# Bias columns by wide products, an earlier iota, and stores on another queue in a two-layer attention kernel

## Chip, cores and metric

The kernel runs on one core of a Trainium2 chip, in one launch. The metric is the device time of that launch in microseconds (us); of several runs the median is taken. Everything is float32.

## What is computed

Two layers follow each other on x, 8 images of 32 x 32 positions with 512 channels (8 x 1024 tokens).

```python
# layer 0
x_norm = group_norm(x) * gn_scale + gn_bias
q, k, v = split(x_norm @ w_qkv + b_qkv)                 # 8 heads of 64
x = x + softmax(q k^T / 64) v @ w_out + b_out
...
# layer 1, on the tokens as 4-dimensional image
q = layernorm(x) @ wq + bq
o = gelu(depthwise_7x7_stride_2(q) + dw_b)              # 16 x 16 points
offsets = pw_w o
interp = bilinear samples of x at (reference points + tanh(offsets))   # 256 rows
v = interp @ wv + bv
k = interp @ wv + bv
qh, kh, vh = q @ mq_w + mq_b, k @ mk_w + mk_b, v @ mv_w + mv_b
z = softmax(qh kh^T) vh @ mo_w + mo_b + x
out = gelu(layernorm(z) @ mlp_w + mlp_b) + z
```

Two matrix products in a row, such as wv and then mk_w, are folded by the kernel into one matrix (wvk = wv mk_w) with one bias. The bias of the folded key product is mk_b + mk_w^T bv, a vector of 512; it is kept as four columns on 128 partitions (512 = 4 x 128). There are three such vectors: bvk (keys: mk_w with bv), bvv (values: mv_w with bv) and bqq (queries: mq_w with bq).

## The kernel before, in words

**Layer 0** goes through 8 batches; a batch has 4 pairs of heads with 8 query tiles each, so 32 units per batch (`per`). A unit (`push`, line 205) makes the scores of one query tile and one pair of heads on TensorE (two PSUM tiles "sc"), their row maxima on VectorE ("nmax"), the exponentials on ScalarE ("e"), and two 32x32-block transposes of them on VectorE into "sq". After every second unit 16 DMAs on SP's queue move "sq" into "et" (`moved`, line 221), and TensorE multiplies "et" by the values some units later ("av"). VectorE scales that by the inverse row sums into "attT".

All other work is put between units by a list of due steps: `at(place, step)` (line 375) enters a step at a place, and `run_due(until)` (line 378) runs all steps due in order of place. It is called twice per unit n: with n + 0.8 after the unit's scores, maxima and exponentials and before its transposes, and with n + 1 after the transposes. `InOrder` keeps every engine's instructions in the order in which they are so recorded: an engine waits at the first instruction that isn't ready. Every instruction recorded this way has line 54 in the profile, so groups are known by their tiles.

Between units lie the next batch's group norm and q, k, v products, the output product of the batch before (`out_steps`, line 703: product with w_out, "xr" as the residual sum, statistics, then layernorm into "hat", stored as hat_d for layer 1), and a part of layer 1: the depthwise convolution, by taps that VectorE adds into "od" and by taps that ScalarE multiplies into two buffers "part_x" and GpSimd adds into "oa" (`conv_chunk`, line 884).

**The last batch (7).** `fold_steps` (line 794) folds the weights. At unit 18.3 `load_biases` (line 429) issues eight loads of small vectors on GpSimd's queue; at 18.4 `set_refs` (line 440) writes partition numbers by an iota on GpSimd and makes reference points of them in eight small VectorE operations. The products for wvk lie at 25.5 to 29.5, for wvv at 30.5 to 32.52, for wqq after the last unit. `add_cols` (line 319) makes the bias columns: for each of 4 output chunks and 4 input chunks one product with a 128x128 weight and a single moving column, 16 products of 128x1, and four ScalarE additions of one column. It is called for bvk at 29.55, for bvv at 35.5 and for bqq at 36.6 (32 is the batch's end).

The last batch's output steps have their own places (`last_places`, line 781): output tiles 0 to 3 are made and normed first, tiles 4 to 7 at 36.2 to 36.35 with norms at 36.84 and after. In this batch the norms run on VectorE (three operations of 128x512 each) and the stores to mid and to hat_d are issued by GpSimd.

**Layer 1** has 16 half batches of 4 pairs of heads. `prep` (line 1062) fetches the first normed tokens, copies two bias vectors for wide products ("rep_w"), gathers the 4 x 2 sets of 128 sample rows of batch 0 by indirect DMAs of GpSimd ("row", four buffers), weighs and adds them on VectorE ("smp"), loads the late weights on SP's queue, and makes the first query product (`query_step(0, 0)`), the keys of four pairs and the values. `unit_steps` (line 1261) then records each unit; 0.042 after unit n stands the query product of unit n + 1.

Three lines show how a wide product is made before, in `project` (line 361), which the rest of the kernel uses: for each of 4 input chunks two halves of 64 output partitions, a moving operand of 512 columns.

```python
for c in range(NC):
    for m in range(2):
        nc.tensor.matmul(out[half], lhsT=lhsT(c)[:, half], rhs=rhs(c), start=(c == 0), stop=(c == NC - 1))
```

Of the kernel before, what the change touches and what calls it, by code (L numbers as in the profile page):

```python
# [9 lines left out]
F32 = mybir.dt.float32  # L10
I32 = mybir.dt.int32
AF = mybir.ActivationFunctionType
ALU = mybir.AluOpType
AX = mybir.AxisListType
# [3 lines left out]
P = 128  # L18
# [3 lines left out]
C = 512  # L22
NC = C // P
NT = S // P
# [223 lines left out]
def attention_then_deformable_attention(  # L248
# [48 lines left out]
    def mm_tile():  # L297
        return ps_mm.tile([P, QB], F32, tag="mm", name="mm")
# [17 lines left out]
        nc.sync.dma_start(t, v.partition_broadcast(P))  # L316
        return t

    def add_cols(dst, w, vec, on_scalar=False):

        n = dst.shape[1]
        ps = mm_tile()
        for o in range(n):
            for c in range(NC):
                nc.tensor.matmul(
                    ps[:, o : o + 1],
                    lhsT=w[:, c, ts(o, P)],
                    rhs=vec[:, c : c + 1],
                    start=(c == 0),
                    stop=(c == NC - 1),  # L330
                )
        if on_scalar:
            for o in range(n):
                col = dst[:, o : o + 1]
                nc.scalar.activation(col, ps[:, o : o + 1], AF.Identity, bias=col)
        else:
            nc.vector.tensor_tensor(dst, ps[:, 0:n], dst, ALU.add)

    def repeat(pool, vec, bufs):

# [34 lines left out]
    def at(place, step):  # L375
        due.append((place, len(due), step))
# [52 lines left out]
    def load_biases():  # L429
        with nc.allow_non_contiguous_dma(reason="small vectors onto partitions"):  # L430
# [4 lines left out]
            for o in range(2):  # L435
                nc.gpsimd.dma_start(
                    pww[:, :, o], pw_w[o].rearrange("(c p) a b -> p (c a b)", p=P)
                )

    def set_refs():  # L440
        nc.gpsimd.iota(pid, pattern=[[0, 1]], base=0, channel_multiplier=1)
        nc.vector.tensor_scalar(rc[:, 0:1], pid, 4, None, ALU.logical_shift_right)
        nc.vector.tensor_scalar(rc[:, 1:2], pid, G - 1, None, ALU.bitwise_and)
        for h in range(2):
            nc.vector.tensor_copy(refs[:, h, :], rc)
        nc.vector.tensor_scalar(refs[:, 1, 0:1], refs[:, 1, 0:1], float(P // G), None, ALU.add)
        nc.vector.tensor_scalar(refs, refs, 0.5, 2.0 / G, ALU.add, ALU.mult)
        nc.vector.tensor_scalar(refs, refs, -1.0, None, ALU.add)
# [61 lines left out]
    with ExitStack() as l0:  # L510
# [192 lines left out]
        def out_steps(b, attT, places, last=False):  # L703

            src = x_tok[b].rearrange("(t p) c -> p t c", p=P)
            dst = mid[b].rearrange("(t p) c -> p t c", p=P)

            room = {}
            to_mid, to_hat = [nc.gpsimd if last else nc.sync] * 2
            by = nc.vector if last else nc.gpsimd

            def row(name, t):

                if last and name == "hat":
                    tag, bufs = ("q", 3) if t < NQT else ("v", 5)
                    return work.tile([P, C], F32, tag=tag, name=name, bufs=bufs)
                if last and t >= NQT + NX:  # L720
                    return (conv["bq"], conv["part"].rearrange("p a s -> p (a s)"))[t % 2]
                if last and t >= NQT:
                    return work.tile([P, C], F32, tag="x", name=name, bufs=NX)
                return work.tile([P, C], F32, tag="xr", name=name, bufs=4)

            def fetch(t):
                room[t] = row("xr", t)
                nc.gpsimd.dma_start(room[t], src[:, t, :])

            def add(t):  # L730
                nc.gpsimd.tensor_tensor(room[t], room[t], bout, ALU.add)

            def out(t):
                room["ps", t] = project(
                    lambda c: attT[c, t // NQT][:, ts(t % NQT, P)], lambda c: room_w["w"][:, c, :]
                )

            def summed(t):
                xr = room[t]
                nc.vector.tensor_tensor(xr, room["ps", t], xr, ALU.add)  # L740
                to_mid.dma_start(dst[:, t, :], xr)
                stats = work.tile([P, 6], F32, tag="stats1", name="stats1", bufs=2)
                mv = room["mv", t] = work.tile([P, 3], F32, tag="mv1", name="mv1", bufs=4)
                nc.vector.bn_stats(stats, xr)
                nc.vector.bn_aggr(mv[:, 0:2], stats)
                rstd(mv[:, 2:3], mv[:, 1:2], 1e-5)

            def norm(t):
                xr, mv = room[t], room["mv", t]
                hat = row("hat", t)  # L750
                nc.vector.tensor_scalar(
                    hat, xr, mv[:, 0:1], mv[:, 2:3], ALU.subtract, ALU.mult
                )
                by.tensor_tensor(hat, hat, lng_row, ALU.mult)
                by.tensor_tensor(hat, hat, lnb_row, ALU.add)
                to_hat.dma_start(hat_d[b][:, t, :], hat)

            for t in range(NT):
                for place, what in zip(places[t], (fetch, add, out, summed, norm)):
                    at(place, lambda t=t, what=what: what(t))  # L760
# [33 lines left out]
        def fold_steps(first):  # L794

            raws, wT = {}, {}

            def spare():
                return work.tile([P, NC, QB], F32, tag="xT", name="raw", bufs=NX_T)

            def fetch(name, w):
                raws[name] = spare()
                nc.gpsimd.dma_start(raws[name], by_chunk(w))

            def turn(name, m):
                if name == "v" and m == 0:
                    wT[name] = spare()
                src = room_w["w"] if name == "v" else raws["wq"]
                ps = mm_tile()
                for c in range(NC):  # L810
                    nc.tensor.transpose(ps[:, ts(c, P)], src[:, c, ts(m, P)], ident)
                nc.scalar.copy(wT[name][:, m, :], ps)

            def product(dst, tag, name, raw, i):
                if i == 0:
                    fold[dst] = kept(tag)
                ps = project(lambda m: wT[name][:, m, ts(i, P)], lambda m: raws[raw][:, m, :])
                nc.scalar.copy(fold[dst][:, i, :], ps)

            at(first + 18.3, load_biases)  # L820
            at(first + 18.4, set_refs)
            at(first + 17.7, lambda: load_weight(wv))
            at(first + 19.3, lambda: fetch("mk", mk_w))
            for m in range(NC):
                at(first + 23.5 + m // 2 + 0.05 * (m % 2), lambda m=m: turn("v", m))
            at(first + 25.3, lambda: load_weight(w_out))
            at(first + 26.7, lambda: fetch("mv", mv_w))
            for i, place in enumerate((25.5, 27.5, 28.5, 29.5)):
                at(first + place, lambda i=i: product("wvk", "wC", "v", "mk", i))
            at(first + 29.55, lambda: add_cols(bvk, raws["mk"], bv_c, on_scalar=True))  # L830
            at(first + 29.7, lambda: fetch("wq", wq))
            for i, place in enumerate((30.5, 31.5, 32.5, 32.52)):
                at(first + place, lambda i=i: product("wvv", "wB", "v", "mv", i))
            last = first + per
            at(last + 0.6, lambda: wT.update(q=spare()))
            at(last + 3.5, lambda: add_cols(bvv, raws["mv"], bv_c, on_scalar=True))
            at(last + 3.6, lambda: fetch("mq", mq_w))
            for m in range(NC):
                at(last + 4.27 + 0.001 * m, lambda m=m: turn("q", m))
            for i in range(NC):  # L840
                at(last + 4.5 + 0.01 * i, lambda i=i: product("wqq", "wA", "q", "mq", i))
            at(last + 4.6, lambda: add_cols(bqq, raws["mq"], bq_c, on_scalar=True))

        def head_steps(first):

# [185 lines left out]
    with ExitStack() as l1:  # L1031
# [30 lines left out]
        def prep():  # L1062
            fetch_hat(0)
            load_small()
            fetch_hat(1)
            reps.extend(repeated(vec) for vec in (bvv, lnb))
            room[0, "ii"], room[0, "wt"] = head["ii"], head["wt"]
            for h in range(2):
                gather(0, h)
                sample(0, h)  # L1070
            for pad in pads:
                nc.gpsimd.memset(pad, 0.0)
            load_late()
            query_step(0, 0)
            for hp in range(NHP):
                key_step(0, hp)
            for t in range(2):
                value_step(0, t)
# [182 lines left out]
        def unit_steps(n):  # L1261
# [20 lines left out]
            last = n + 1 == 2 * B * NHP  # L1282
            at(n + (1.3 if last else 1.1), lambda: att.product(u))
            at(n + (1.305 if last else 1.2), scale)
            if not last:
                at(n + 0.042, lambda: query_step(*divmod(n + 1, NHP)))


# [114 lines left out]
```

## Time and profile before

| | us |
|---|---|
| three runs: lowest, median, highest | 3339.33, 3346.2, 3357.7 |
| the profiled execution's own time | 3348.16 |
| its span in the profile | 3346.5 |
| TensorE busy | 3273.1 |
| VectorE busy | 2494.1 |
| ScalarE busy | 1809.5 |
| GpSimd busy | 1544.3 |
| mean granted clock of TensorE | 0.993 of full speed |

How to read what is shown below. A timeline row has the start in us from the span's start, the time that a run of like instructions took, the engine, the line, the operation, output<-input by tile names, partitions x elements, and how many; in square brackets stands how long the engine had been idle before, and what ended that wait. One float32 product is two records of TensorE, so 16 records are the 8 instructions of one wide product. A row by stretches begins with the stretch, then its length, and the busy time and number of instructions of PE, PEld (weight loads), DVE, ACT and POOL; the three last columns are the granted TensorE clock, the share of the DMA engines and GB/s. "SPq" is SP's DMA queue. A wait for several semaphores is put down to the one that came last.

### The profile page before, as it was taken

To read this page: it belongs to the slowest core of one execution; us is meant where nothing else is said; L and a number is where in the kernel's file an instruction comes from. 1 tells how busy PE (TensorE), PEld (TensorE's weight loads), DVE (VectorE), ACT (ScalarE), POOL (GpSimd) and SP (SyncE) were. 2 spreads that over 40 slices of the span, in tenths; PEclk is the share of its full clock that TensorE was granted. 3 is DMA by queue.
4 is the path that set the end of the run, shared out by engine and by line. 5 is a ranking of instruction groups with operands and counts; after the bars stand their busy time and mean duration, and the time that the engine had idled before them with its cause. 6 is when DMAs were issued, how large, how long until landed. Compare 5 with 4: busy or idle time off the path is not lost.

```text
span 3346.5 us, 59638 instructions
## 1 busy us (share of the span) xinstructions
PE 3273.1 (98%) x21736; PEld 1337.3 (40%) x21736; DVE 2494.1 (75%) x3389; ACT 1809.5 (54%) x3927; POOL 1544.3 (46%) x1909
## 2 busy tenths in 40 slices
PE   7999999999999999999999999999999999999998
PEld 3344444344344344444444434433333333333333
DVE  5777788888898898888888877448767686665754
ACT  3443356576566567567567555135565555554442
POOL 1001226746745764764664663415455454642222
PEclk9999999999999999999999999999999999999999
DMA  5666766766776777766776767567566665665754
GB/s 151 176 181 163 209 181 180 232 180 181 208 202 180 214 195 183 208 193 184 212 193 176 201 185 214 163 196 221 185 208 202 192 201 189 212 216 191 226 181 130
DMA packets 441412, 643.61 MB, mean 192 GB/s; under 512 B 73152, under 2 KB 236992, under 8 KB 439072
## 3 DMA queue, kind: packets, MB, share of 16 engines
q1 hardware_dynamic: 409232, 531.93, 55.2%
q0 software_dynamic: 31888, 107.88, 10.5%
q8 instruction: 172, 2.82, 0.4%
q14 instruction: 120, 0.98, 0.1%
HBM read 247.43 MB, written 123.73 MB: 111 GB/s over the span
## 4 chain that ended last, share of the span: by engine, by line
PE 85%; ACT 4%; DVE 3%; DMA 3%; POOL 2%; issue 2%; SPq 1%; POOLq 0%; DVEq 0%; ACTq 0%
PE mm L54 54%; PE sc L54 16%; PE av L54 15%; ACT e L54 2%; SPq L54 1%; DMA et<-sq 1%; DVE nmax L54 1%; DVE sq L54 1%; POOL chunk L54 1%; DMA inv<-rs_d 1%; POOL xr L54 1%; DMA row<-mid,ii 0%; ACT L54 0%; DMA w<-in_L_conv_w_out_dram 0%; DVE smp L54 0%
## 5 line engine op out<-in xcount | busy, mean ns | idle before, releaser
L54 ACT ACTIVATE e<-sc,nmax 128x1024 f32<-128x1024 f32 (+1 forms) x1024 | 803.0, 797 | 480.9 <-DVE nmax L54 479.2
L54 DVE TENSOR_REDUCE nmax<-sc 128x1 f32<-128x1024 f32 (+1 forms) x640 | 751.5, 1215 | 344.5 <-PE sc L54 343.9
L54 POOL TENSOR_TENSOR oa<-part_x,oa 128x256 f32<-128x256 f32 x852 | 640.4, 752 | 553.7 <-ACT part_x L54 507.5
L54 DVE STREAM_TRANSPOSE sq<-e 128x1024 f32<-128x1024 f32 x640 | 766.2, 1228 | 156.8 <-ACT e L54 135.7
L54 ACT ACTIVATE part_x<-pad_x,dww_x 128x256 f32<-128x256 f32 x852 | 441.2, 545 | 259.4 <-POOL oa L54 257.9
L54 PE MATMUL sc<-k,q 64*64 64x512 f32 x4096 | 516.1, 605 | 15.8 <-ACT e L54 13.7
L54 PE MATMUL av<-et,v 128*64 128x256 f32 x4096 | 499.2, 386 | 6.2 <-DMA et<-sq 3.8
L54 PEld LDWEIGHTS av<-et,v 128*64 128x64 f32 x4096 | 273.4, 137 | 324.1 <-issue 164.5
L54 POOL TENSOR_TENSOR chunk<-parts,chunk 128x256 f32<-128x256 f32 x240 | 189.2, 788 | 259.3 <-ACT parts L54 245.3
L54 POOL TENSOR_TENSOR mv<-mv,minus_half 128x1 f32<-128x1 f32 x128 | 76.4, 597 | 462.8 <-DVE mv L54 462.0
L54 PEld LDWEIGHTS sc<-k,q 64*64 64x64 f32 x4096 | 139.4, 133 | 322.5 <-issue 208.4
L54 PE MATMUL mm<-xT,wB 128*64 128x512 f32 x1024 | 233.0, 597 | 3.2 <-issue 3.2
L54 DVE SCALAR_TENSOR_TENSOR od<-pad_x,dww_x,od 128x256 f32<-128x256 f32 x276 | 231.5, 839 | 5.5
L54 PE MATMUL mm<-wo,attH 128*64 128x512 f32 x1024 | 233.7, 598 | 0.0
L54 PE MATMUL mm<-w,attT 128*64 128x512 f32 x1024 | 232.5, 598 | 0.8 <-DMA w<-in_L_conv_w_out_dram 0.8
L54 PE MATMUL mm<-hat_h,wA 128*64 128x512 f32 x1024 | 232.9, 597 | 0.0
L54 PE MATMUL mm<-wC,xT 128*64 128x256 f32 x2048 | 232.1, 379 | 0.0
L54 PE MATMUL mm<-wm,zT 128*64 128x512 f32 x1024 | 230.7, 592 | 1.0 <-ACT zT L54 1.0
L54 PE MATMUL mm<-xT,wA 128*64 128x512 f32 x1024 | 230.7, 592 | 0.0
L54 ACT ACTIVATION_READ_ACCUMULATOR e<-sc,nmax 128x1 f32 x1024 | 209.2, 204 | 0.0
L54 ACT ACTIVATE parts<-pad,dww 128x256 f32<-128x256 f32 x240 | 126.5, 552 | 126.6 <-POOL chunk L54 125.6
L54 PEld LDWEIGHTS mm<-wC,xT 128*64 128x64 f32 x2048 | 148.1, 137 | 77.6 <-issue 6.4
(185 smaller groups left out, 3501.6 us busy)
## 6 DMA issues: line engine op xcount, KB each, us to landing
et<-sq SPq DMA_DIRECT2D x2048, 128.0 KB, 2.8
sq_d<-sq SPq DMA_DIRECT2D x128, 512.0 KB, 2.7
et<-sq_d SPq DMA_DIRECT2D x128, 512.0 KB, 4.5
inv<-rs_d SPq DMA_DIRECT2D x256, 128.0 KB, 4.6
hat_h<-hat_d SPq DMA_DIRECT2D x16, 1024.0 KB, 8.7
xr<-mid SPq DMA_DIRECT2D x64, 256.0 KB, 5.9
xr<-in_x_dram POOLq DMA_DIRECT2D x62, 256.0 KB, 3.9
x<-in_x_dram POOLq DMA_DIRECT2D x60, 256.0 KB, 4.5
```

The costliest lines, as they stand in the source:

```text
L54: return self.tc.keep_in_program_order(op(*args, **kwargs))
```

## The change

Four things are edited.

1. The iota gets a step of its own, `number`, at 18.3, ahead of the bias loads (now 18.35); the VectorE part, `set_refs`, goes to 19.3.
2. `add_cols` is replaced by `add_diagonal`. The two vectors bv and bq are each repeated over 128 columns by one VectorE copy (`repeats`, at 27.9; a tile [128, 8, 128] in the buffer of "hat_x"). A bias is then one wide product (`project`) of the repeated vector with the weight: every one of the 128 output rows holds all 512 values. VectorE multiplies it by the identity, repeated four times, into "own" (a "v" buffer), sums each block of 128 into "col", and adds that to the bias.
3. The stores of the last batch's normed tiles 4 to 7 are issued by ScalarE instead of GpSimd.
4. The query product of layer 1's unit 1 is recorded in `prep`, behind that of unit 0 and ahead of the keys, and left out after unit 0.

```diff
-    def add_cols(dst, w, vec, on_scalar=False):
-
-        n = dst.shape[1]
-        ps = mm_tile()
-        for o in range(n):
-            for c in range(NC):
-                nc.tensor.matmul(
-                    ps[:, o : o + 1],
-                    lhsT=w[:, c, ts(o, P)],
-                    rhs=vec[:, c : c + 1],
-                    start=(c == 0),
-                    stop=(c == NC - 1),
-                )
-        if on_scalar:
-            for o in range(n):
-                col = dst[:, o : o + 1]
-                nc.scalar.activation(col, ps[:, o : o + 1], AF.Identity, bias=col)
-        else:
-            nc.vector.tensor_tensor(dst, ps[:, 0:n], dst, ALU.add)
+    def add_diagonal(pool, dst, w, rep):
+
+        out = project(lambda c: rep[:, c, :], lambda c: w[:, c, :])
+        own = pool.tile([P, C], F32, tag="v", name="own", bufs=5).rearrange("p (o q) -> p o q", q=P)
+        nc.vector.tensor_tensor(
+            own, out.rearrange("p (o q) -> p o q", q=P),
+            ident.unsqueeze(1).to_broadcast([P, NC, P]), ALU.mult,
+        )
+        col = pool.tile([P, NC], F32, tag="mu", name="col", bufs=2)
+        nc.vector.tensor_reduce(col, own, AX.X, ALU.add)
+        nc.vector.tensor_tensor(dst, col, dst, ALU.add)
...
+    def number():
+        nc.gpsimd.iota(pid, pattern=[[0, 1]], base=0, channel_multiplier=1)
+
     def set_refs():
-        nc.gpsimd.iota(pid, pattern=[[0, 1]], base=0, channel_multiplier=1)
...
-                to_hat.dma_start(hat_d[b][:, t, :], hat)
+                (nc.scalar if last and t >= NQT else to_hat).dma_start(hat_d[b][:, t, :], hat)
...
+            def repeats():
+                both = work.tile([P, NT, P], F32, tag="hat_x", name="rep_b", bufs=1)
+                for half, vec in enumerate((bv_c, bq_c)):
+                    rep = raws["rep", half] = both[:, ts(half, NC), :]
+                    nc.vector.tensor_copy(rep, vec.unsqueeze(2).to_broadcast([P, NC, P]))
...
-            at(first + 18.3, load_biases)
-            at(first + 18.4, set_refs)
+            at(first + 18.3, number)
+            at(first + 18.35, load_biases)
+            at(first + 19.3, set_refs)
+            at(first + 27.9, repeats)
...
-            at(first + 29.55, lambda: add_cols(bvk, raws["mk"], bv_c, on_scalar=True))
+            at(first + 29.55, lambda: add_diagonal(work, bvk, raws["mk"], raws["rep", 0]))
...
-            at(last + 3.5, lambda: add_cols(bvv, raws["mv"], bv_c, on_scalar=True))
+            at(last + 3.5, lambda: add_diagonal(work, bvv, raws["mv"], raws["rep", 0]))
...
-            at(last + 4.6, lambda: add_cols(bqq, raws["mq"], bq_c, on_scalar=True))
+            at(last + 4.6, lambda: add_diagonal(work, bqq, raws["mq"], raws["rep", 1]))
...
             query_step(0, 0)
+            query_step(0, 1)
...
-            if not last:
+            if not last and n:
                 at(n + 0.042, lambda: query_step(*divmod(n + 1, NHP)))
```

## The prediction

> **What bounds the kernel now.** I read the busy table and the chain's shares first, then the timelines of TensorE (PE), VectorE (DVE), GpSimd (POOL) and ScalarE (ACT) around the edited steps (1.98 to 2.24 ms), then the granted clock by stretch.
>
> ```profile
> span 3346.5 us, 59638 instructions
> PE 3273.1 (98%) x21736; PEld 1337.3 (40%) x21736; DVE 2494.1 (75%) x3389; ACT 1809.5 (54%) x3927; POOL 1544.3 (46%) x1909
> ...
> PE 85%; ACT 4%; DVE 3%; DMA 3%; POOL 2%; issue 2%; SPq 1%; POOLq 0%; DVEq 0%; ACTq 0%
> ```
>
> TensorE is busy 98% of the span, so an edit counts only by what it does to TensorE's work, its idle stretches and its clock. All edits lie in the last batch of the first layer and the step to the second. There TensorE has two long idle stretches:
>
> ```profile
> 2003.50 4.30 PE L54 MATMUL sc<-k,q 64*64 64x512 f32 x16 [7.19 <-ACT e L54]
> ...
> 2185.42 9.84 PE L54 MATMUL mm<-smp,wC 128*64 128x256 f32 x60 [5.53 <-DVE smp L54]
> ```
>
> The first goes back over ScalarE's exponentials to VectorE, which waits for the iota behind eight bias loads:
>
> ```profile
> 1983.83 2.35 DVE L54 TENSOR_REDUCE nmax<-sc 128x1 f32<-128x1024 f32 x2 [0.33 <-PE sc L54]
> 1996.03 0.21 DVE L54 TENSOR_SCALAR rc<-pid 128x1 int32<-128x1 int32 x2 [9.85 <-POOL pid L54]
> ...
> 1994.35 1.49 POOL L54 DMA_DIRECT2D pww<-in_L_conv_pw_w_dram  x2
> 1995.84 0.15 POOL L54 IOTA pid<- 128x1 int32 x1
> ...
> 1996.72 0.53 ACT L54 ACTIVATE part_x<-pad_x,dww_x 128x256 f32<-128x256 f32 x1 [6.10 <-POOL oa L54]
> 2002.24 1.11 ACT L54 ACTIVATE e<-sc,nmax 128x1024 f32<-128x1024 f32 x1 [4.99 <-DVE nmax L54]
> ```
>
> The third thing to see is the clock (next to last columns: granted clock as a share, DMA share). TensorE is "busy" in the 128x1 products, yet the clock falls to half in and after them:
>
> ```profile
> 2075.66 3.60 PE L54 MATMUL mm<-raw 128*64 128x512 f32 x16
> 2079.19 4.24 PE L54 MATMUL mm<-bv_c,raw 128*128 128x1 f32 x32
> 2083.36 3.69 PE L54 MATMUL sc<-k,q 64*64 64x512 f32 x16
> 2086.98 2.96 PE L54 MATMUL av<-et,v 128*64 128x256 f32 x16
> ...
> 2079.20:2083.40 4.20, 4.20 (x38) 4.19 (x36) 0.00 (x0) 0.59 (x1) 0.00 (x0) 0.86 0.68 163
> 2083.40:2087.00 3.60, 3.60 (x19) 0.78 (x18) 0.00 (x0) 0.71 (x4) 1.84 (x3) 0.50 0.83 162
> ```
>
> **Part 1: iota ahead, refs one unit later.** The iota issues at about 1989.9, where the loads began (its 0.15 us goes ahead of their 5.96). VectorE no longer waits; what is late next? Its first conv tap into "od" needs the previous store of that tile, issued 1984.08 and landed 8.6 us later, at 1992.7. Two taps and the row maximum then end at 1994.7. But ScalarE's exponential stands behind a conv tap (1996.72) that waits for GpSimd's adds, still behind the same loads: it ends at 1997.4. So the first exponential runs 1997.4 to 1998.4 and TensorE resumes at 1998.45 instead of 2003.50: idle 2.2 us, not 7.2. The scores that follow ran at clock 0.58 and took 4.30 us; after an idle of 1.89 us (at 2064.8) the trace shows the usual 1.95, so I take full clock. They still need the second exponential (1999.55), so they end near 2001.3 instead of 2007.8, 6.5 earlier. The refs' eight small operations (1.7 us) now stand between maxima and transposes, where VectorE waits for the exponential anyhow; but three taps ahead of the next maxima delay its second exponential to 2007.4 where TensorE wants it at 2006.9, 0.5 lost. **Net -6.0**; bounds -7.4 (all idle but 2.2, full clock) and 0 (rival 2).
>
> **Part 2: bvk by a wide product.** 32 narrow records take 4.17 us to the next start (2079.19 to 2083.36); the same weights' wide product of 16 records takes 3.53 (2075.66 to 2079.19): 0.64 less. The products after it took 3.62 and 2.79 instead of 1.87 and 1.78, 2.8 more by the clock. Face value -3.4. But the diagonal is summed on VectorE, and in the changed order its three operations stand **ahead of the unit's two transposes**. They wait for the product's end, 2082.7. Masked multiply as other PSUM additions of 128x512 (0.69), reduction as half of a 1024-wide maximum (0.6), addition 0.16, gaps: 1.6 us. The transposes thus end at 2086.8 instead of 2078.94. Sixteen et<-sq transfers are queued on SP behind them; they were issued 2079.00 to 2090.36 and would end issuing near 2098.2, the last landing at 2100.4 to 2102.4 (2.8 to 4.8 from issue to landing, medians of the page and of 2100-2104). TensorE, now earlier, asks for them at 2097.4; before it began that product at 2100.87. So about 3.7 us of new idle, and the product begins at 2101.1: +0.2 in place of -3.4. An idle of 3.7 lies between 1.89 (no drop) and 5.53 (drop to 0.50); nearest in kind are the narrow products, where the clock fell after 2.5 to 3.2 us of thin work. I take a drop, 2.4 us (4.30 against 1.9 above). **Net +2.6**; bounds -3.4 (transfers in time) and +4.3 (last landing, 2.8 by the clock).
>
> [...]
>
> **Part 3: bvv, bqq, the stores and the early query, one chain.** Times are those of before, shifted as a whole by parts 1 and 2. Narrow bvv costs 4.59 us and 2.3 of slow clock after; wide 3.53. Its column sum now stands on VectorE ahead of the last attT scaling (which moves from 2132.8 to 2136.7; the output product needs it for its last quarter at 2137, so no idle) and of four norms (1.91 each). The norms' delay reaches back through the residual sums to TensorE by less than 1 us, so the wqq products start some 2.2 us earlier than 2155.0 and bqq's product ends at 2170.5 instead of 2173.8.
>
> Here is the new wait. Before, the four later norms ran 2156.97 to 2164.7, while TensorE made wqq:
>
> ```profile
> 2164.61 0.42 DVE L54 COPY rep_w<-bvv 128x512 f32<-128x512 f32 x1
> ...
> 2169.88 0.48 DVE L54 TENSOR_SCALAR smp<-row,wt 128x512 f32<-128x512 f32 x1 [4.51 <-DMA row<-mid,ii]
> ...
> 2184.61 0.75 DVE L54 SCALAR_TENSOR_TENSOR smp<-row,wt,smp 128x512 f32<-128x512 f32 x1 [0.96 <-DMA row<-mid,ii]
> ```
>
> Now bqq's column sum stands ahead of them and waits for 2170.5. Behind it: sum 1.6, norms 7.64, two copies 0.76, so sampling starts at 2180.6 instead of 2169.88. That POOL is free of the four stores lets only the first gather go early; the second is behind a buffer that the first norm reads. All four first-half rows are there by 2180.6, but the second four need their buffers back (2181.1 to 2183.5), are issued 2181.4 to 2185.3 at 1.3 apart, and the last lands 3.4 (first gather of before) to 8.2 us (its last, beside the weight loads) later. Those loads shift too: SP's first waits for the last norm's input and two others for ScalarE's stores. I take 5.7: sampling ends at 2191.8, TensorE's key products start 6.3 late (bounds 4.0 and 8.8). The query product put ahead, 3.53 us, fills idle time: -3.53. Later its absence is felt: it stood between the first scores and the first output product, which now comes 14.4 us after those scores began, while its second et landed 16.1 after them (2218.2 less 2202.05): +1.7. The slow restart (clock 0.50) is there in both. ScalarE's four stores hold back its query evacuations to 2180.6, ahead of the keys; an issue there is not in the trace, SP's 0.34 and POOL's 0.55 bound it, and it hides. **Net +4.5**, bounds -1.8 (sampling no later) and +7.1.
>
> **Sum.** -6.0 + 2.6 + 4.5 = +1.1 us on the profiled execution's 3348.16 (span 3346.5 and 1.7 around it), which stands 2.0 above the median of three, 3346.2. Forecast **3347**.
>
> **Rivals.**
> 1. *The column sums' queueing on VectorE decides* (slower). Place: norms and sampling behind bqq's sum, transposes behind bvk's. Price: +7.1 and +4.3, with the first stall's clock still dropping (-6.0 becomes -3.6): +7.8, 3354. It decides once the last gather lands over 6 us after issue and both idles drop the clock. For it: 8.2 measured beside the loads; against: these have partly drained by then. 0.25.
> 2. *The moved iota does nothing*: the chain names a late et<-sq as what released the transposes at 1997.95. Against it: the same kind of transpose started at 1970.44 amid its predecessor's transfers. Then 0 + 2.6 + 4.5: 3353. 0.10.
> 3. *The new waits hide*, savings stay: -6.0 - 3.4 - 1.8 = -11.2, 3335. For it: transfers of 2.8 us, earlier first gather; against: the queue order. 0.13.
>
> **How the numbers follow.** Likeliest 0.52. All cases lie within 0.4%; this kernel's measurement tells about 0.5% (17 us) from no change, and the three runs span 18 us. Range by the parts' bounds: 3334 (-12.6) to 3357 (+11.4). Faster 0.03, same 0.93, slower 0.04.
>
> **What would show it.** Right: idle before the scores near 2003 falls to about 2 us; VectorE waits some 6 us for TensorE ahead of the bvk sum and 15 us ahead of bqq's; TensorE idles ahead of an av product on et<-sq, and over 12 us ahead of the keys. Wrong: no such idle (rival 3), the 7 us still there (rival 2), or a shift in the second layer's steady units, where I expect none.

## The result, and the profile after

| kernel | median, us (runs) | lowest, highest | ratio to before, 95% interval |
|---|---|---|---|
| before | 3345.15 (20) | 3339.33, 3357.7 | |
| changed | 3354.53 (20) | 3344.81, 3360.48 | 1.0026 [1.0017, 1.0035] |

The change costs 9.4 us by the medians, 0.26%. The profiled execution of the changed kernel took 3351.23 us; it lies 3.3 below its kernel's median, and that of before (3348.16) lies 3.0 above its own. So the two traces, compared below, show a difference of 3.1 us where the medians show 9.4.

From the profile of the changed kernel: the span, the busy table and the shares of the chain of work that ended last, by engine.

```profile
span 3349.5 us, 59538 instructions
...
PE 3268.0 (98%) x21688; PEld 1328.8 (40%) x21688; DVE 2498.3 (75%) x3400; ACT 1806.6 (54%) x3915; POOL 1539.6 (46%) x1905
...
PE 86%; DVE 3%; ACT 3%; DMA 2%; POOL 2%; issue 2%; SPq 1%; POOLq 0%; ACTq 0%; DVEq 0%
```

TensorE is busy 5.1 us less (3273.1 before), and the span is 3.0 longer: the time went into idle stretches. The timeline of TensorE in the changed kernel shows which:

```profile
1997.81 3.04 PE L54 MATMUL sc<-k,q 64*64 64x512 f32 x16 [2.06 <-ACT e L54]
...
2061.25 3.36 PE L54 MATMUL av<-et,v 128*64 128x256 f32 x16 [2.54 <-DMA et<-sq]
...
2097.56 3.68 PE L54 MATMUL av<-et,v 128*64 128x256 f32 x16 [3.83 <-DMA et<-sq]
...
2168.75 7.04 PE L54 MATMUL mm<-hat_h,wA 128*64 128x512 f32 x32
2181.80 1.12 PE L54 MATMUL mm<-smp,wC 128*64 128x256 f32 x4 [6.01 <-DVE smp L54]
2191.60 8.48 PE L54 MATMUL mm<-smp,wC 128*64 128x256 f32 x60 [8.68 <-DVE smp L54]
```

The idle of 7.19 us before the scores is 2.06 now. In its place stand 3.83 us ahead of an output product, which did not exist before, and 14.69 us (6.01 and 8.68) ahead of the key products, where there were 5.53. VectorE's timeline says what it did meanwhile:

```profile
2078.99 0.69 DVE L54 TENSOR_TENSOR own<-mm,ident 128x512 f32<-128x512 f32 x1 [6.38 <-PE mm L54]
...
2168.97 0.69 DVE L54 TENSOR_TENSOR own<-mm,ident 128x512 f32<-128x512 f32 x1 [15.34 <-PE mm L54]
2169.69 0.69 DVE L54 TENSOR_REDUCE col<-own 128x4 f32<-128x512 f32 x1
2170.41 0.16 DVE L54 TENSOR_TENSOR bqq<-col,bqq 128x4 f32<-128x4 f32 x1
2170.50 0.54 DVE L54 TENSOR_SCALAR hat<-xr,mv 128x512 f32<-128x512 f32 x1
...
2178.81 0.48 DVE L54 TENSOR_SCALAR smp<-row,wt 128x512 f32<-128x512 f32 x1
...
2190.79 0.75 DVE L54 SCALAR_TENSOR_TENSOR smp<-row,wt,smp 128x512 f32<-128x512 f32 x1 [0.36 <-DMA row<-mid,ii]
```

VectorE stands still for 15.34 us, until TensorE has made the bqq product, and only then begins the four norms ("hat<-xr,mv"), whose inputs were complete by 2154.3. Sampling ("smp") follows the norms. GpSimd, too, waits for them, though its stores are gone from its queue:

```profile
2154.96 1.07 POOL L54 DMA_INDIRECT row<-mid,ii  x1 [0.49 <-issue]
2171.31 1.31 POOL L54 DMA_INDIRECT row<-mid,ii  x1 [15.28 <-DVE hat L54]
...
2184.03 0.95 POOL L54 DMA_INDIRECT row<-mid,ii  x1 [0.30 <-issue]
```

The first gather goes at once; the second needs a buffer that the first norm reads, and waits 15.28 us for it. In the kernel before, the gathers stood behind the four stores, and the first went later than the changed kernel's first, but earlier than its second:

```profile
2166.48 1.05 POOL L54 DMA_INDIRECT row<-mid,ii  x1 [0.70 <-issue]
```

Along TensorE's timeline the shift against before (negative: the changed kernel is earlier) is -0.6 us at the last scores that no edit can have touched (1989.04 to 1988.47), -6.9 at the output product after the first stall (2007.73 to 2000.79), -3.8 at the scores of 2072.01 (2068.25), -0.9 at the output product of 2109.51 (2108.66), +4.0 at layer 1's third scores (2228.64 to 2232.60), and +3.1 at the end. The first and the last but one of these places, in the timelines of before and then of the changed kernel:

```profile
1989.04 1.95 PE L54 MATMUL sc<-k,q 64*64 64x512 f32 x16
...
2228.64 1.96 PE L54 MATMUL sc<-keys,q 64*64 64x256 f32 x32
```

```profile
1988.47 1.95 PE L54 MATMUL sc<-k,q 64*64 64x512 f32 x16
...
2232.60 1.96 PE L54 MATMUL sc<-keys,q 64*64 64x256 f32 x32
```

What lies between them is called the edited stretch below. It is 4.5 us longer in the changed kernel's trace.

### The profile page after: what moved, and what is told of

Read it like the earlier page. It is cut to its first block, busy times and chain, and to the rows that moved or that the text cites. A ratio compares the mean times of both kernels' runs of the same rounds, so it can differ in the third digit from the quotient of the medians.

```text
span 3349.5 us, 59538 instructions
## 1 busy us (share of the span) xinstructions
PE 3268.0 (98%) x21688; PEld 1328.8 (40%) x21688; DVE 2498.3 (75%) x3400; ACT 1806.6 (54%) x3915; POOL 1539.6 (46%) x1905
## 3 DMA queue, kind: packets, MB, share of 16 engines
q0 software_dynamic: 31568, 106.83, 10.4%
## 4 chain that ended last, share of the span: by engine, by line
PE 86%; DVE 3%; ACT 3%; DMA 2%; POOL 2%; issue 2%; SPq 1%; POOLq 0%; ACTq 0%; DVEq 0%
PE mm L54 54%; PE sc L54 16%; PE av L54 16%; ACT e L54 2%; SPq L54 1%; POOL chunk L54 1%; DMA et<-sq 1%; DVE nmax L54 1%; DVE sq L54 1%; DMA inv<-rs_d 1%; POOL xr L54 0%; ACT L54 0%; DVE smp L54 0%; DMA et<-sq_d 0%; POOL res L54 0%
```

## The experiments

Theory A: VectorE takes its instructions in order (in the changed kernel it stood 15.34 us at bqq's sum with four norms behind it whose inputs were complete), so the place of the column sums decides; ahead of the transposes (bvk) and of the norms (bqq) they cost more than the earlier iota brings. Rivals: the stores on ScalarE's queue and the early query cost the time; the moved iota gives its gain back; the clock alone makes the difference.

All measured, each against before on the same chip (differences of medians). The last column is from the traces: how much longer the edited stretch is than in the profile of before. It rests on one execution of each kernel, but what happens in the rest of the program does not enter it.

| kernel | us against before | ratio, 95% interval | edited stretch, us |
|---|---|---|---|
| refs only | -7.5 | 0.9979 [0.9969, 0.9988] | -9.0 |
| wide products only | +18.9 | 1.0054 [1.0041, 1.0067] | +15.2 |
| stores and early query only | -11.7 | 0.9964 [0.9951, 0.9977] | -8.3 |
| changed, bqq's sum behind the norms, bvk's behind the transposes | -0.5 | 0.9992 [0.9983, 1.0001] | -11.5 |
| changed, with the narrow products of before | -14.9 | 0.9950 [0.9937, 0.9963] | -17.6 |
| changed, both sums behind (bqq's behind the first sampling) | -19.2 | 0.9939 [0.9926, 0.9952] | -19.1 |
| the same, bvk's sum ahead | -15.2 | 0.9953 [0.9940, 0.9966] | -15.8 |
| changed, again | +4.3 | 1.0018 [1.0004, 1.0032] | +7.0 |
| both sums behind, without the early query | -19.6 | 0.9943 [0.9928, 0.9958] | -18.8 |
| wide products only, both sums behind | -1.7 | 0.9998 [0.9989, 1.0007] | -7.0 |
| both sums behind, again | -18.2 | 0.9945 [0.9932, 0.9957] | -19.3 |
| stores only | -8.9 | 0.9972 [0.9960, 0.9984] | -10.9 |

Median and trace agree within 4 us, but for two kernels: the first attempt at placing the sums (-0.5 and -11.5) and the wide products with both sums behind (-1.7 and -7.0). The profiled execution of each of these two is the shortest of its kernel (as it is of three others). For the changed kernel's first comparison the two are +9.4 and +4.5.

### Each part alone

**Refs only.** Before, with

```diff
-            at(first + 18.3, load_biases)
-            at(first + 18.4, set_refs)
+            at(first + 18.3, number)
+            at(first + 18.35, load_biases)
+            at(first + 19.3, set_refs)
```

> The kernel before with the first part of the change alone: iota ahead of the bias loads, refs one unit later. Theory A (the change loses its time because the column sums stand ahead of other VectorE work; the moved iota itself gains): about 6 us less than before (ratio 0.998), idle before the scores near 2003 about 2 us instead of 7.2. Rival R1 (the moved iota is itself followed by a clock drop that takes half of its gain back, as the drop near 2061 in the changed kernel's profile suggests): about 3 us less. Rival R2 (medians of this kernel wander by 6 us with the clock, whatever is edited): no sign of its own, between -6 and +6 us.

Measured -7.5 us: theory A, and not half of it as R1 had. The idle ahead of the scores is 2.06 us here as well.

**Wide products only.** Before, with `add_diagonal` and `repeats` in the places that the change gives them.

> The kernel before with the three bias columns as wide products alone (iota, stores and second query as before). Theory A: slower, by +2.6 us at bvk and about +6 at the keys (VectorE's norms and sampling behind bqq's sum, no early query to fill the idle), less some 2 us for bvv: +5 to +9 us, with TensorE idle over 12 us ahead of the key products. Rival R3 (the stores on ScalarE's queue and the early query bring the loss): this kernel is faster, -3 to -6 us, by the shorter products and the full clock after them.

Measured +18.9: the sign is A's, the size more than twice what it said. GpSimd's and TensorE's timelines of this kernel show what was left out of the sum:

```profile
2172.54 0.58 POOL L54 DMA_DIRECT2D hat_d<-hat  x1 [18.46 <-DVE hat L54]
...
2178.27 0.54 POOL L54 DMA_DIRECT2D hat_d<-hat  x1 [1.37 <-DVE hat L54]
2178.80 0.26 POOL L54 MEMSET rs<- 128x32 f32 x2
2179.76 1.04 POOL L54 DMA_INDIRECT row<-mid,ii  x1 [0.70 <-issue]
```

```profile
2190.69 1.12 PE L54 MATMUL mm<-smp,wC 128*64 128x256 f32 x4 [18.59 <-DVE smp L54]
2199.15 9.17 PE L54 MATMUL mm<-smp,wC 128*64 128x256 f32 x60 [7.34 <-DVE smp L54]
```

With the stores still on GpSimd's queue, every gather stands behind four stores, which stand behind four norms, which stand behind the column sum. The first gather goes at 2179.76 (before: 2166.48), and TensorE idles 25.9 us ahead of the keys.

**Stores and early query only.** Before, with

```diff
-                to_hat.dma_start(hat_d[b][:, t, :], hat)
+                (nc.scalar if last and t >= NQT else to_hat).dma_start(hat_d[b][:, t, :], hat)
...
             query_step(0, 0)
+            query_step(0, 1)
...
-            if not last:
+            if not last and n:
```

> The kernel before with the four stores by ScalarE's queue and the second query ahead of the keys alone (narrow products kept). Theory A: -3.5 us (the query fills idle time) +1.7 (the first output product then waits for its et): about -2 us, the keys no later than before. Rival R3 (the stores or the early query bring the loss): +3 to +6 us, with the query evacuations late and the keys behind them.

Measured -11.7: R3 falls, and A's -2 is far too small. Which of the two edits carries it, the **stores only** kernel (the first line of this diff) tells:

> The kernel before with one edit: the four late stores of normed tokens by ScalarE's queue. Theory A3 (formed after the runs so far: with norms that are not held back, the stores on GpSimd's queue are what stands ahead of the gathers; moved away, the first gather goes behind the statistics of the last tile, some 5 us earlier): the stores carry most of the -11.7 us that they and the early query gave together, -7 to -12 us against before, and under 2 us of idle ahead of the keys in place of 5.5 and more. Rival R10 (the early query carries it, by filling the idle): 0 to -4 us, with the idle ahead of the keys as long as before.

Measured -8.9 us: the stores carry most of it (A3). Its GpSimd and TensorE timelines:

```profile
2159.24 1.52 POOL L54 DMA_INDIRECT row<-mid,ii  x1 [0.34 <-issue]
2161.06 0.97 POOL L54 DMA_INDIRECT row<-mid,ii  x1 [0.31 <-DVE hat L54]
```

```profile
2180.14 7.42 PE L54 MATMUL mm<-smp,wC 128*64 128x256 f32 x64
```

Where the norms are not held up, the gathers start 7.2 us earlier than before (2166.48), beside the norms, and TensorE goes into the key products without a pause. Whether the early query adds to this is not shown: the medians differ by 2.8 with overlapping intervals, and in the traces the edited stretch is 2.6 us longer with it (-8.3 against -10.9).

### The place of the sums

**First attempt.** The changed kernel, with the product where it was and the sum in a step of its own:

```diff
-            at(first + 29.55, lambda: add_diagonal(work, bvk, ...))
+            at(first + 29.55, lambda: raws.update(p_bvk=wide(raws["mk"], raws["rep", 0])))
+            at(first + 29.85, lambda: add_diagonal(work, bvk, raws["p_bvk"]))
...
-            at(last + 4.6, lambda: add_diagonal(work, bqq, ...))
+            at(last + 4.6, lambda: raws.update(p_bqq=wide(raws["mq"], raws["rep", 1])))
+            at(last + 4.95, lambda: add_diagonal(work, bqq, raws["p_bqq"]))
```

> The changed kernel with the same wide products in the same places, but two column sums later on VectorE: bvk's behind the unit's two transposes, bqq's behind the four norms. Theory A: the idle ahead of the output product near 2097 goes, the norms run beside the wqq products again and sampling starts near 2171 instead of 2179; about -3.4 at bvk and -6 to -8 at the keys against the changed kernel's own terms: 8 to 14 us below before (3331 to 3337). Rival R4 (the time is lost to clock drops that come with any earlier arrival at a DMA-bound product, not to the sums' place): within 3 us of the changed kernel, +3 to +9 us above before.

Measured -0.5, between the two. In the trace, which is of the shortest of twelve executions (3341.26 us, the median is 3348.76), the edited stretch is 11.5 us shorter, which lies within what A said; what the other executions lose was not shown. VectorE's and TensorE's timelines show a wait that A had not seen:

```profile
2160.01 0.69 DVE L54 TENSOR_TENSOR own<-mm,ident 128x512 f32<-128x512 f32 x1 [7.55 <-PE mm L54]
...
2162.41 0.48 DVE L54 TENSOR_SCALAR smp<-row,wt 128x512 f32<-128x512 f32 x1
```

```profile
2176.35 8.35 PE L54 MATMUL mm<-smp,wC 128*64 128x256 f32 x60 [9.07 <-DVE smp L54]
```

The norms are free, but the first sampling still stands behind the sum, and that behind TensorE. The wait had only moved down the queue by one step; 9.07 us of idle ahead of the keys stayed.

**Behind the first sampling.** As the last, but bqq's sum goes into layer 1's `prep`:

```diff
             for h in range(2):
                 gather(0, h)
                 sample(0, h)
+                if h == 0:
+                    add_diagonal(work, bqq, fold["p_bqq"], "xr", 4)
```

> The changed kernel with the same wide products, bvk's sum behind the unit's two transposes and bqq's behind the first half's sampling instead of ahead of the norms. In the run with bqq's sum just behind the norms, VectorE still waited 7.55 us for bqq's product ahead of the first sampling, and TensorE 9.07 us ahead of the keys. Theory A2: that wait goes, sampling starts some 8 us earlier, the idle ahead of the keys falls under 2 us: 7 to 9 us less than that run's kernel, -8 to -10 us against before. Rival R6 (the rows' transfers, not the sum, end the second half's sampling): within 2 us of it, 0 to -2.

Measured -19.2 us, and -18.2 on another occasion:

> The kernel with both sums behind once more, on another occasion: -17 to -23 us against before, if its first comparison was no luck; A2 and its rivals agree here.

VectorE's and TensorE's timelines of this kernel:

```profile
2152.93 0.48 DVE L54 TENSOR_SCALAR smp<-row,wt 128x512 f32<-128x512 f32 x1
2153.45 2.33 DVE L54 SCALAR_TENSOR_TENSOR smp<-row,wt,smp 128x512 f32<-128x512 f32 x3
2159.89 0.69 DVE L54 TENSOR_TENSOR own<-mm,ident 128x512 f32<-128x512 f32 x1 [4.12 <-PE mm L54]
...
2164.91 0.75 DVE L54 SCALAR_TENSOR_TENSOR smp<-row,wt,smp 128x512 f32<-128x512 f32 x1 [0.29 <-DMA row<-mid,ii]
```

```profile
2159.67 7.04 PE L54 MATMUL mm<-hat_h,wA 128*64 128x512 f32 x32
2166.53 7.42 PE L54 MATMUL mm<-smp,wC 128*64 128x256 f32 x64
2173.79 7.04 PE L54 MATMUL mm<-wB,smp 128*64 128x512 f32 x32
```

VectorE now waits for the product between the two halves of sampling, while the second half's rows are under way. Sampling ends at 2165.66, before TensorE is through with the two queries, so TensorE has no idle at all ahead of the keys. By the medians the gain is more than A2 said (-8 to -10, counted from the -0.5 of the first attempt). In the traces the step from the first attempt is 7.6 us (-11.5 to -19.1), within A2's 7 to 9; the rest is the distance between the first attempt's median and its trace. This kernel is faster than before and than the changed one; it differs from the latter by the place of two sums alone.

**bqq's sum only**, bvk's left ahead of the transposes:

> As the last, but bvk's sum stays ahead of the unit's two transposes, as in the changed kernel. Theory A2: the idle of 3.8 us near 2097 on an et transfer stays, and a clock drop in part of the executions: 4 to 7 us more than with both sums behind. Rival R7 (an idle at bvk is given back at a later wait of the same chain): within 2 us of the kernel with both behind.

Measured -15.2, 3.9 more than with both behind; the intervals overlap, so the time alone would not settle it. TensorE's timelines do, first of this kernel, then of the one with both behind:

```profile
2094.33 2.69 PE L54 MATMUL av<-et,v 128*64 128x256 f32 x16 [3.60 <-DMA et<-sq]
```

```profile
2090.94 1.95 PE L54 MATMUL av<-et,v 128*64 128x256 f32 x16 [0.31 <-DVE attT L54]
```

The idle on an et transfer is there with bvk's sum ahead and gone with it behind. Of the 23.5 us between the changed kernel (3352.6 in this comparison) and both sums behind (3329.1), bqq's place is 19.6. The traces of the same comparison say 26.1 and 22.8, those of the changed kernel's first profile 23.6 and 20.3.

### What is left when the sums are placed

**Changed, with the narrow products of before** (all else as changed):

> The changed kernel with the three bias columns as in the kernel before (narrow products, summed by ScalarE), all else changed. Theory A2 (the sums on VectorE ahead of the norms also hold back the gathers, which start behind the first norm; without them the refs' gain and that of the stores and the query simply add): -7.5 - 11.7, about -19 us against before, no long idle ahead of the key products. Rival R5 (the gains are of one kind, each only ends a wait that the other would end): no better than the better of the two, about -12 us.

Measured -14.9, by the ratio's interval -12.4 to -21.1: both theories lie in or at it, so the times leave open whether the two gains add in full. In the traces they do: the edited stretch is 9.0 us shorter with the refs alone, 8.3 with the stores and the query, and 17.6 with both. With both sums behind, the wide products are 4.3 us faster than this, with overlapping intervals.

**Wide products only, both sums behind** (iota, stores and second query as before):

> The kernel before with only the wide products, both sums behind (iota, stores on GpSimd's queue and second query as before). Theory A2 (what made the wide products alone cost 19 us is the place of the sums, and no other thing): the 18.6 us of idle ahead of the keys falls to before's 5 or 6, and the products' own gain is left, 0.6 to 1.5 each and the clock after them, about -6 to -9 us against before. Rival R9 (the wide products bring the keys' wait in any order as long as GpSimd's queue holds the stores ahead of the gathers): +2 to +8 us.

Measured -1.7: both missed. The sums' place explains all of the 19 us, but in the median next to nothing of the products' own gain came through. GpSimd's and TensorE's timelines:

```profile
2157.42 0.54 POOL L54 DMA_DIRECT2D hat_d<-hat  x1 [1.37 <-DVE hat L54]
2157.95 0.26 POOL L54 MEMSET rs<- 128x32 f32 x2
2158.91 1.04 POOL L54 DMA_INDIRECT row<-mid,ii  x1 [0.70 <-issue]
```

```profile
2178.27 8.67 PE L54 MATMUL mm<-smp,wC 128*64 128x256 f32 x60 [9.60 <-DVE smp L54]
```

TensorE is there earlier and waits longer, 9.60 us instead of 5.53, for gathers that stand behind the stores. So 4.1 us of what the shorter products saved ahead of that wait are given back at it. The rest is not: in this trace, of the shortest of eleven executions (3344.04 us), the edited stretch is still 7.0 us shorter than before, which is what A2 said. Why the median gains only 1.7 stays open.

**Both sums behind, without the early query:**

> The kernel with both sums behind, but with the second query after the first scores again, as before. In the kernel with both sums behind, TensorE has no idle ahead of the keys (two queries, 2159.7 to 2166.5, and sampling ends at 2165.7), and 2.6 us of idle on et transfers in the first output product of the second layer, with the clock down after it. Theory A2 (the early query fills idle time only where there is some): without it the keys start 0.7 us earlier, after some 2.5 us of idle, and the later idle goes: -2 to 0 us against the kernel with both sums behind (which is run again beside it). Rival R8 (the early query is a gain of 3.5 us wherever it stands): +3 to +4 us.

Measured 3330.1, beside 3331.6 with the early query. The six times without it reach from 3323.1 to 3338.3, so the medians alone do not exclude R8; the traces do. From the start of bqq's product to layer 1's third scores TensorE takes 50.3 us without the early query (2159.46 to 2209.73), and 50.5 and 53.0 with it (2156.30 to 2206.81, and 2156.24 to 2209.22 in the earlier profile of the same kernel). Without it TensorE idles 2.38 us ahead of the keys; with it, 1.7 us ahead of the first output product (2.6 in the earlier profile). It fills an idle stretch only where there is one. (The edited stretch as a whole, -18.8 without it and -19.3 or -19.1 with it, also holds a loss near 2062 us in the trace without it, behind 2.77 us of idle, which the other two do not have there.)

### The changed kernel again

> The changed kernel itself once more, as the measure for the others on this chip, and for a second profile of it. If the 6 us between its median and its first profiled execution come from clock drops that only some executions have, its times spread over 10 us or more again, and a slow profile shows more stretches of half clock after idle stretches than the first; if the first profile was typical, the ratio falls to about 1.001.

Measured 1.0018 [1.0004, 1.0032]; 12 runs from 3346.3 to 3369.7. (The 6 us of this text are what is left of the medians' +9.4 when the profiles' +3.1 is taken off; 3.3 of them lie between the changed kernel's median and its first profile.) The second profile (3353.44 us) is 2.2 us longer than the first, and it loses that at the key products:

```profile
2192.30 9.72 PE L54 MATMUL mm<-smp,wC 128*64 128x256 f32 x60 [9.60 <-DVE smp L54]
```

The idle ahead of them is 9.60 us instead of 8.68, and the products take 9.72 us instead of 8.48, with the clock down for longer (0.81 over them in the first profile; about 0.7 here, an estimate: 0.81 x 8.48 / 9.72). The last gather was used 7.7 us after its issue here (2183.80 to 2191.49), and 6.8 us after it in the first (2184.03 to 2190.79). A part of the difference between these two executions, then, is when the last rows arrive.

Another profile shows a loss in a place that no edit touches. TensorE in the stores-only kernel:

```profile
1930.60 3.68 PE L54 MATMUL av<-et,v 128*64 128x256 f32 x16 [3.51 <-DVE rs L54]
1934.04 4.83 PE L54 MATMUL mm<-xT,wB 128*64 128x512 f32 x16
```

At this output product the profile of before has 0.1 us of idle. Here it has 3.51, the clock falls to 0.50 after it, and 6.3 us are lost in all (the shift against before goes from -2.5 to +3.8). The kernel with the stores and the early query lost 6.3 us in the same way one batch earlier (3.32 idle at 1670.05, clock 0.50 from there to 1675); the other ten profiles of this section, and those of before and of the changed kernel, show no such loss there. So an execution can lose some 6 us by chance (6.3 in both traces); what sets this off was not followed up. The twelve times of the first attempt at the sums fit such losses (five from 3341.3 to 3344.3, seven from 3348.7 to 3350.7), and so does the changed kernel's median, 3.3 above its first profile; that it is them was not shown.

## Why the prediction was right, and where not

Forecast 3347.0 (range 3334 to 3357, within 0.5% at 0.93); measured 3354.53, inside the range, 0.26% slower. The steps that it named came true in the traces:

- **Part 1** (net -6.0): idle 2.06 ahead of the scores where about 2 was expected; of the shift of -6.9 behind the first stall 0.6 stood there ahead of every edit, and the next scores lost 0.4 (2.39 us instead of 1.95; expected 0.5), so -5.9 in all. Made alone it gave -7.5 us (-4.0 to -10.4 by the interval). Rival 2 falls.
- **Part 2** (net +2.6): VectorE waited 6.38 us (expected 6), TensorE then idled 3.83 (expected 3.7), and the clock fell to 0.50 (over 2097.5 to 2101.0) as assumed. From 2072 to 2109 us the shift goes from -3.8 to -0.9, +2.9.
- **Part 3** (net +4.5): sampling began 9.9 us after bqq's product ended (expected 10.1); the key products began at 2191.6, 7.0 late against the shift of -0.9 that parts 1 and 2 had left (expected 6.3); the early query gave 3.6 back; the first output product waited 1.4 (expected 1.7). From 2109 to 2229 the shift grows by 4.8. That this is so near to 4.5 is partly luck, for three misses nearly cancel: the keys were 0.7 later than expected, their slow restart, taken to be the same, was 1.4 shorter (8.48 us against 9.84), and the early query's later absence cost 2.7 in all (1.4 of it as idle), not 1.7. Rival 3, that the new waits hide, falls.
- Layer 1's later units shift by no more than 0.9 us, as expected.

Not in the sum: a clock drop at 2061.25 (0.57 over 2061.2 to 2064.3) after an idle of 2.54 us, 1.7 us. With it the sum is +2.8, and the profile's difference is +3.1. That they lie so near is luck in part as well: no term holds the 0.65 us more of idle at that place (1.89 before), the 0.6 by which the changed kernel's execution was ahead when the edits began, or the 0.9 that it regained late in layer 1. The rest up to the medians' +9.4 lies between executions, and the forecast had only one profile of before, 3.0 above its kernel's median. The median equals the price of rival 1 (3354), and part of that rival's condition was met (the last gather was used 6.8 us after its issue), but its own sign, a clock drop at the first stall, was not seen: the granted clock there was 1.00. The changed kernel's second profile comes closer to that rival: the last gather was used 7.7 us after its issue, and the edited stretch is 7.0 us longer than before. Theory A, that the place of the sums decides, is the mechanism of both the likeliest case and rival 1; they differ in sizes.

**What the prediction mis-sized** is behind its net terms. It priced the queueing against the kernel before and found +2.6 and +4.5. Against the same kernel with two sums placed later the queueing costs 23.5 us. The difference is a gain that the change brought and the queueing ate at once: the prediction said that freeing GpSimd of the four stores "lets only the first gather go early", which is what happened, but the stores' move is worth 8.9 us where the norms are not held up. And the early query, priced at -3.53 and +1.7, gave 3.6 back and cost 2.7 in the changed kernel's trace; where TensorE has no idle ahead of the keys, the traces show no gain from it between bqq's product and layer 1's third scores.

## What to carry to other kernels

Where an engine takes its instructions in order, a short operation that waits for another engine costs what stands behind it: put a consumer behind the work that is ready, and follow that down the queue, since one step further may hold the same wait (here 9.07 us of idle ahead of the keys with the sum one step further back, and none with it behind the first sampling). A gain ahead of a wait that another chain ends can be given back at it (4.1 us in the kernel with the wide products alone, both sums behind); look at what ends that wait, too. A change that measures 0.26% may hold large effects of both signs; make its parts one by one. And where one program's times scatter by more than the effect, compare medians and traces, and say where they disagree.

## What the runs showed of the hardware

The length of a short idle stretch did not say whether the clock drops. Windows of the changed kernel just after its idle stretches of 2.06 and 2.54 us (the granted clock is the third column from the right):

```profile
1997.80:2000.80 3.00, 2.97 (x18) 0.70 (x18) 3.00 (x4) 2.52 (x6) 1.28 (x2) 1.00 0.01 3
2061.20:2064.30 3.10, 3.05 (x16) 2.22 (x18) 2.61 (x4) 1.22 (x3) 0.00 (x0) 0.57 0.86 199
```

And of the kernel with the refs alone, just after its idle stretches of 2.06 and 2.54 us in the same places:

```profile
1996.60:2000.50 3.90, 3.82 (x16) 0.79 (x16) 3.83 (x5) 3.42 (x8) 2.06 (x3) 0.76 0.02 4
...
2060.90:2062.60 1.70, 1.70 (x16) 1.38 (x18) 1.51 (x3) 1.14 (x3) 0.00 (x0) 1.00 0.77 195
```

The same two lengths, with the drop at the one in one execution (0.57 behind 2.54 us, 1.00 behind 2.06) and at the other in the other (0.76 behind 2.06 us, 1.00 behind 2.54): in these traces an idle of 2 to 2.5 us dropped the clock or did not, and its length alone did not decide. In the changed kernel's second profile a gap of 2.04 us was followed by a drop (clock 0.71 over 2060.5 to 2063). The stretches of half clock in the changed kernel's trace after its first 30 us lasted 3.4, 6.8, 13.7 and 3.4 us (from 2061.6, 2095.8, 2181.1 and 2266.4 us on). What decided where they came was not shown.

In or behind the narrow products (128x1) the clock fell although TensorE counts as busy in them. In the profile of before it is 0.86 in bvk's (2079.2 to 2083.4) and 0.50 behind them, 0.78 in bvv's (2130.9 to 2135.5) and 0.50 behind them, 0.72 in bqq's (2168.8 to 2173.9) and 0.65 behind them (to 2179.5). It fell 3.0, 2.5 and 2.1 us after their first records, where the prediction has 2.5 to 3.2. In the changed kernel, with wide products for bvv and bqq, it stays at 1.00 from 2102.7 to 2181.0 us. Where in the products the drop came varied: bvk's 32 records took 4.24 us before, and 3.73 us at full clock with the refs alone, where the drop came just behind them (0.53 over 2077 to 2080.6).
